# The entries of two graph attentions: a first block of 256 nodes, and Newton's steps of the later blocks on POOL

## The chip, the cores and the metric

The kernel runs on one core of a Trainium2 chip. The metric is the device time of one execution, in microseconds (us); less is better. Five engines work side by side, each through its own list of instructions in order: PE (matmuls), DVE (vector), ACT (activations), POOL (GpSimd) and SP, which here only starts transfers. Between engines there are semaphores. Transfers are started from the queues of SP, ACT and POOL.

## The reference

Four layers, each a graph attention and a feed-forward network, on 2708 nodes of 256 numbers, in float32, with one adjacency matrix for all. The change concerns the graph attentions of layers 2 and 3, which have one head:

```
xn = layernorm(x)                      # per node: mean, variance, 1/sqrt(var + 1e-5)
Wh = xn @ W (+ bias in layer 2)        # 2708 x 256
e  = leaky_relu((Wh @ a1)[:, None] + (Wh @ a2)[None, :], 0.2)
x  = x + softmax(where(adj > 0, e, -9e15)) @ Wh        # elu of it in layer 3
```

The x that enters has just received the results of a mixture of experts: in layer 1 each node is sent to one expert of eight, in layer 2 to two. Their results lie in device memory, and are fetched and added to x, weighted, before the layer norm can start.

## The kernel before

x stays in SBUF as X, 22 tiles of 128 nodes (the last has 20). Both attentions are made by one function, `gat_single` (from L1163). It has an **entry**, which makes everything that the pairs of nodes need, and then the long loop over pairs (`gat_pairs`, L664, and the matmuls of L1311). This loop can start only when the entry has ended, since each of its steps reads `big_p`, a row over all nodes. I call the entry of layer 2 the first entry (tiles `fys`, `g2...`) and that of layer 3 the second (tiles `dys`, `g3...`).

The entry works on six blocks, `chunks(512)`: five of four tiles and one of two (148 nodes). For each block:

- `combine` (L1689) has started the loads of all blocks at the beginning, one transfer `y` for each block and choice (512 KB; whole tiles and the short last tile apart), alternately from SP's and POOL's queue, and for the first block's second choice from ACT's. It then adds the results tile by tile on DVE (L1715): one instruction for each tile in the first entry, two in the second. It is a generator; each `next` adds one block.
- `Stats.sums` (L136): `bn_stats` and `bn_aggr` on DVE for each tile; if asked, ACT's square root of the block's variances (L147). `Stats.roots` (L150) is the reciprocal that follows on DVE.
- `Stats.newton` (L153) makes the inverse root on DVE instead: `inverse_root` (L307) with three instructions for a first guess and three rounds of three (L320 to L322). It is used for blocks 2 and 3 together, and for 4 and 5 together, since ACT has gone from square roots to exponentials by then.
- `norm` (L1191): one DVE instruction for each tile, x minus mean, times rstd, into `f` (L108).
- `project` (L1197): PE transposes the tiles by pairs (L1207), ACT copies them into `ft` and sums them (L1213), PE multiplies by W (L123, `pv`), ACT takes two exponentials of the last column (L1226, L1227), and the 256 columns are scaled into V, by ACT in blocks 0 to 3 (L1229) and by DVE in 4 and 5 (L1232). Then PE makes the row of scores for the block (L1235, `s1p`) and ACT its exponential (L1238, `big_p`).

The order on DVE is written out by hand: `turn` makes each step's instructions follow the last one of the step before (`tc.issue_after`). It is: add 0; sums 0; add 1; roots 0; norm 0; sums 1; add 2; (project 0); roots 1; norm 1; (project 1); sums 2; add 3; sums 3; newton 2+3; norm 2, project 2, norm 3, project 3; add 4; add 5; sums 4+5; newton 4+5; norm 4; norm 5; project 4; project 5. At the end a sum over all nodes (L1283) and a row of V for nodes with no neighbour (L1288, L1289).

POOL has little to do in an entry: it starts its loads, and later it clears a part of the next layer's weights `w` and starts a few loads of weights (L1381, L1766, L93), in the second entry it clears and starts the masks (L2250, L2245) and two loads (L93, L86).

Of the kernel before, what the change touches and what calls it, by code (L numbers as in the profile page):

```python
# [16 lines left out]
P = 128  # L17
N = 2708
# [25 lines left out]
def chunks(width):  # L44

    return [(c, min(width, N - c)) for c in range(0, N, width)]


def tiles_of(start, length):
# [254 lines left out]
        nc.vector.tensor_scalar(net.empty, den, 0.0, None, ALU.is_equal)  # L304


def inverse_root(net, pool, v, scale, eps, name, out=None):  # L307


    nc = net.nc  # L310
    n = v.shape[1]
    x = pool.tile([P, n], F32, name=f"{name}x")
    nc.vector.tensor_scalar(x, v, scale, eps, ALU.mult, ALU.add)
    half = pool.tile([P, n], I32, name=f"{name}h")
    nc.vector.tensor_scalar(half, x.bitcast(I32), 1, None, ALU.logical_shift_right)
    y = pool.tile([P, n], F32, name=f"{name}y") if out is None else out
    nc.vector.tensor_scalar(y.bitcast(I32), half, -1.0, float(0x5F3759DF), ALU.mult, ALU.add)
    t = pool.tile([P, n], F32, name=f"{name}t")
    for _ in range(3):
        nc.vector.scalar_tensor_tensor(t, y, -0.5, y, ALU.mult, ALU.mult)  # L320
        nc.vector.tensor_tensor(t, t, x, ALU.mult)
        last = nc.vector.scalar_tensor_tensor(y, t, 1.5, y, ALU.add, ALU.mult)  # L322
    return y if out is None else last
# [839 lines left out]
def gat_single(net, key, head, feed, elu):  # L1163
# [7 lines left out]
    with ExitStack() as ctx:  # L1171
# [7 lines left out]
        nc.vector.memset(ratio[:, LAST:], 0.0)  # L1179

        nc.scalar.activation(small.tile([P, 1], F32, name="warm", bufs=1), net.ln_eps, AF.Sqrt)
        blocks = chunks(512)
        parts = big.tile([P, NT // 2, 2], F32, name="parts")
        ln = Stats(net)
        with ExitStack() as c1:
# [11 lines left out]
            def project(n):  # L1197
                n0, nw = blocks[n]
                its = tiles_of(n0, nw)
                ft = work.tile([P, 2, 512], F32, name="ft")  # L1200
                for k in range(0, len(its), 2):
                    pair = its[k : k + 2]
                    ps = psum.tile([P, 2, 2 * P], F32, name="tp")
                    for m, t in enumerate(pair):
                        r, f = rows(t), fs.pop(t)
                        for c in range(2):
                            nc.tensor.transpose(  # L1207
                                ps[:, c, m * P : m * P + r], f[:r, c * P : (c + 1) * P], net.ident[:r, :r]
                            )
                    pw = (len(pair) - 1) * P + rows(pair[-1])  # L1210

                    for c in range(2):
                        nc.scalar.activation(  # L1213
                            ft[:, c, k * P : k * P + pw],
                            ps[:, c, :pw],
                            AF.Copy,
                            accum_out=parts[:, 2 * n + k // 2, c : c + 1],
                        )
                    for m, t in enumerate(pair):
                        r = rows(t)  # L1220
                        pv = psum.tile([P, D + 1], F32, name="pv", bufs=3)
                        net.matmul_k(pv[:r], ft[:, :, (k + m) * P : (k + m) * P + r], w)
                        low = V[:r, t, D : D + 1]

                        with tc.issue_after(ln.root.ins) if t == 0 else nullcontext():
                            nc.scalar.activation(low, pv[:r, D:], AF.Exp, scale=SLOPE)  # L1226
                        nc.scalar.activation(ratio[:r, t : t + 1], pv[:r, D:], AF.Exp, scale=1.0 - SLOPE)  # L1227
                        if n < 4:
                            nc.scalar.activation(V[:r, t, :D], pv[:r, :D], AF.Copy, scale=low)  # L1229
                        else:  # L1230
                            with tc.issue_after(last.ins):
                                nc.vector.tensor_scalar(V[:r, t, :D], pv[:r, :D], low, None, ALU.mult)  # L1232
                ps = psum.tile([P, 512], F32, name="s1p")
                for c in range(2):
                    nc.tensor.matmul(  # L1235
                        ps[:, :nw], a1[:, c, :].to_broadcast([P, P]), ft[:, c, :nw], start=c == 0, stop=c == 1
                    )
                nc.scalar.activation(  # L1238
                    big_p[:, n0 : n0 + nw], ps[:, :nw], AF.Exp, scale=1.0 - SLOPE, bias=0.0 if bias is None else head.grow
                )  # L1240

            def tiles(n0, n1):
                return tiles_of(*blocks[n0])[0], tiles_of(*blocks[n1])[-1] + 1
# [10 lines left out]
            def add():  # L1254
                return next(rest, None)

            turn(add)
            turn(ln.sums, *tiles(0, 0))
            turn(add)
            turn(ln.roots, *tiles(0, 0))  # L1260
            turn(norm, 0)
            turn(ln.sums, *tiles(1, 1))
            turn(add)
            project(0)
            turn(ln.roots, *tiles(1, 1))
            turn(norm, 1)
            project(1)
            turn(ln.sums, *tiles(2, 2), root=False)
            turn(add)
            turn(ln.sums, *tiles(3, 3), root=False)  # L1270
            turn(ln.newton, small, *tiles(2, 3))
            for n in (2, 3):
                turn(norm, n)
                project(n)
            turn(add)
            turn(add)
            turn(ln.sums, *tiles(4, 5), root=False)
            turn(ln.newton, small, *tiles(4, 5))
            for n in (4, 5):
                turn(norm, n)  # L1280
            for n in (4, 5):
                project(n)
            nc.vector.tensor_reduce(fsum, parts.rearrange("p n c -> p c n"), AX.X, ALU.add)  # L1283

            one_row = slice(SPARE, SPARE + 1)
# [113 lines left out]
class Routing:  # L1399
# [288 lines left out]

    def combine(self, pool):  # L1689

        net, nc, X = self.net, self.net.nc, self.net.X
        loaded = []
        queues = nc.sync, nc.gpsimd
        for n, (n0, nw) in enumerate(chunks(512)):
            its = tiles_of(n0, nw)
            ys = []
            for c in range(self.choices):
                y = pool.tile([P, 4, D], F32, name=f"y{c}", bufs=len(chunks(512)))
                for k0, k1, r in whole_and_rest(its):
                    r0 = (c * NT + its[k0]) * P  # L1700

                    engine = nc.scalar if n == 0 and c else queues[(n + c) % 2]
                    read = engine.dma_start(
                        y[:r, k0:k1, :],
                        self.ys[r0 : r0 + (k1 - k0 - 1) * P + r, :].rearrange("(t p) d -> p t d", p=r),
                    )
                    if engine is nc.gpsimd:
                        self.read = read
                ys.append(y)
            loaded.append((its, ys))  # L1710
        for its, ys in loaded:
            for k, t in enumerate(its):
                r = rows(t)
                for c, y in enumerate(ys):
                    last = nc.vector.scalar_tensor_tensor(  # L1715
                        X[:r, t, :], y[:r, k, :], self.weight[:r, c, t : t + 1], X[:r, t, :], ALU.mult, ALU.add
                    )
            yield last


def attention(net, route, ln2, router, weights, mixture):
# [629 lines left out]
```

## Time and profile before

| | us |
|---|---|
| runs of the kernel before: median of 3 (lowest, highest) | 2817.94 (2809.52, 2823.55) |
| the profiled execution | 2806.95 |
| its span in the trace | 2805.2 |
| first entry: first add on DVE to first matmul of the pairs | 1350.55 to 1399.70 |
| second entry: the same | 2499.97 to 2551.70 |

| busy over the whole span | PE | DVE | ACT | POOL |
|---|---|---|---|---|
| share | 93% | 52% | 37% | 13% |

PE's share says that the kernel as a whole is bound by PE; the two entries together take about 101 us of the span, and an entry has its own limits: it begins with PE empty, as all of PE's work hangs on additions and layer norms that DVE has to do first. A line of the chain of waits reads: start, duration, what. In a list of instructions the tile that is written stands left of the arrow, those read right of it, then the shape, the count, and in brackets how long the engine was idle before, and whose end it waited for.

### The profile page before, as it was taken

To read this page: it belongs to the slowest core of one execution; us is meant where nothing else is said; L and a number is where in the kernel's file an instruction comes from. 1 tells how busy PE (TensorE), PEld (TensorE's weight loads), DVE (VectorE), ACT (ScalarE), POOL (GpSimd) and SP (SyncE) were. 2 spreads that over 40 slices of the span, in tenths; PEclk is the share of its full clock that TensorE was granted. 3 is DMA by queue.
4 is the path that set the end of the run, shared out by engine and by line. 5 is a ranking of instruction groups with operands and counts; after the bars stand their busy time and mean duration, and the time that the engine had idled before them with its cause. 6 is when DMAs were issued, how large, how long until landed. Compare 5 with 4: busy or idle time off the path is not lost.

```text
span 2805.2 us, 32369 instructions
## 1 busy us (share of the span) xinstructions
PE 2603.2 (93%) x11710; PEld 1611.2 (57%) x11710; DVE 1454.0 (52%) x3102; ACT 1040.9 (37%) x1641; POOL 377.2 (13%) x470
## 2 busy tenths in 40 slices
PE   5999999798999999969799989999989999969998
PEld 4667746574333444558588743333346777757885
DVE  7753348543777776332554456554664222255555
ACT  3444443314565662321444322233332222234453
POOL 1000012100000001134130013323331111110002
PEclk9999999787999999989899999999999999989999
DMA  8899420000000002654310010000121111040001
GB/s 294 287 290 304 149 69 1 3 5 1 1 1 1 1 1 85 173 168 133 108 33 1 1 36 23 18 1 24 77 99 64 35 33 33 25 168 33 1 1 40
DMA packets 106874, 197.70 MB, mean 70 GB/s; under 512 B 8846, under 2 KB 63736, under 8 KB 103876
## 3 DMA queue, kind: packets, MB, share of 16 engines
q1 hardware_dynamic: 88010, 146.82, 16.9%
q0 software_dynamic: 14896, 43.89, 4.8%
q10 hardware_dynamic: 3806, 4.85, 0.6%
q8 instruction: 99, 1.62, 0.2%
q14 instruction: 63, 0.52, 0.1%
HBM read 135.82 MB, written 59.71 MB: 70 GB/s over the span
## 4 chain that ended last, share of the span: by engine, by line
PE 77%; DVE 8%; issue 5%; DMA 4%; ACT 3%; POOL 2%; SPq 0%; ACTq 0%; POOLq 0%; DVEq 0%
PE acc L1311 15%; PE acc L805 8%; PE acc L284 7%; PE h L2031 7%; PE den L816 4%; PE po L2063 4%; PE po L1872 4%; PE score L273 3%; PE sc L1852 3%; PE pv L123 3%; PE h L943 2%; PE sc L1818 2%; PE po L123 2%; DMA dys<-y,to 2%; PE pl L123 1%
## 5 line engine op out<-in xcount | busy, mean ns | idle before, releaser
L675 DVE SCALAR_TENSOR_TENSOR e<-e,mask 128x768 f32<-128x768 f32 (+2 forms) x264 | 412.1, 1576 | 304.4 <-ACT e L674 304.3
L674 ACT ACTIVATE e<-big_p,minus_one,ratio 128x768 f32<-128x768 f32 (+2 forms) x264 | 394.8, 1513 | 367.0 <-PE acc L1311 229.8
L1311 PE MATMUL acc<-V,e 128*128 128x257 f32 (+1 forms) x1936 | 433.5, 383 | 4.5 <-DVE e L675 4.4
L1311 PEld LDWEIGHTS acc<-V,e 128*128 128x128 f32 (+1 forms) x1936 | 352.3, 186 | 85.7 <-issue 32.1
L805 PE MATMUL acc<-e,V 128*64 128x512 f32 (+1 forms) x1056 | 242.7, 548 | 4.4 <-DVE e L675 4.4
L2031 PE MATMUL h<-w,ft 128*128 (+1 forms) x752 | 234.1, 453 | 0.5 <-DVE dso_far L1497 0.5
L284 PE MATMUL acc<-F,e 128*128 128x257 f32 x968 | 226.3, 384 | 3.0 <-DVE e L281 2.6
L284 PEld LDWEIGHTS acc<-F,e 128*128 128x128 f32 x968 | 173.4, 185 | 66.9 <-DVE e L281 28.4
L805 PEld LDWEIGHTS acc<-e,V 128*64 128x64 f32 x1056 | 107.9, 137 | 161.8 <-issue 129.2
L1852 PE MATMUL sc<-qt,kt 64*128 64x512 f32 (+5 forms) x568 | 170.1, 566 | 4.1 <-ACT e L1866 2.4
L2048 DVE TENSOR_TENSOR hh<-hh,h 128x682 f32<-128x682 f32 x47 | 40.7, 865 | 247.5 <-PE h L2031 247.5
L2031 PEld LDWEIGHTS h<-w,ft 128*128 128x128 f32 x752 | 135.9, 191 | 56.5 <-issue 1.8
L1866 ACT ACTIVATE e<-sc 128x1024 f32<-128x1024 f32 (+4 forms) x121 | 100.2, 857 | 183.1 <-PE sc L1852 167.8
L281 DVE TENSOR_TENSOR e<-e,mask 128x512 f32<-128x512 f32 (+2 forms) x132 | 80.4, 625 | 149.0 <-ACT e L275 147.3
L1878 DVE TENSOR_TENSOR sum<-sum,e 128x1024 f32<-128x1024 f32 (+5 forms) x95 | 104.7, 1102 | 74.5 <-ACT e L1866 71.2
L2063 PE MATMUL po<-w,ht 114*128 (+1 forms) x564 | 131.6, 383 | 5.3 <-DVE ht L2056 5.3
L275 ACT ACTIVATE e<-score 128x512 f32<-128x512 f32 (+2 forms) x132 | 69.7, 544 | 179.0 <-PE score L273 152.1
L1872 PE MATMUL po<-e,V 128*64 128x512 f32 (+4 forms) x484 | 112.3, 542 | 17.5 <-DVE e L1870 9.0
L816 PE MATMUL den<-e,low 128*3 128x512 f32 (+1 forms) x1056 | 123.8, 542 | 0.3 <-DVE e L675 0.3
L2063 PEld LDWEIGHTS po<-w,ht 114*128 114x128 f32 x564 | 107.5, 191 | 27.8 <-DVE ht L2056 12.9
L273 PE MATMUL score<-QK 128*128 128x512 f32 (+2 forms) x264 | 112.1, 554 | 1.2 <-ACT e L275 0.7
L1852 PEld LDWEIGHTS sc<-qt,kt 64*128 64x128 f32 (+1 forms) x568 | 58.4, 188 | 89.3 <-issue 74.0
(639 smaller groups left out, 3463.3 us busy)
## 6 DMA issues: line engine op xcount, KB each, us to landing
row<-in_adj SPq DMA_DIRECT2D x21, 1354.0 KB
raw<-in_adjT SPq DMA_DIRECT2D x35, 768.0 KB
hs<-zero SPq DMA_DIRECT2D x8, 2838.0 KB
hidden<-hr SPq DMA_DIRECT2D x32, 256.0 KB
wd<-in_f_wd SPq DMA_DIRECT2D x8, 1024.0 KB
kept<-mask SPq DMA_DIRECT2D x21, 338.5 KB
mask<-kept SPq DMA_DIRECT2D x21, 338.5 KB
w<-in_d_w1T SPq DMA_DIRECT2D x8, 682.0 KB
```

Of the source, the lines that this page charges most:

```text
L123: self.nc.tensor.matmul(out, lhsT[:, c, :], rhs[:, c, :], start=first and c == 0, stop=last and c == n - 1)
L273: nc.tensor.matmul(ps[:r, :iw], QK[:, 0, span(j)], QK[:, 1, i0 : i0 + iw], start=True, stop=True)
L284: nc.tensor.matmul(acc[k][:ri], e[:r, k * P : k * P + ri], F[:r, j, :], start=j == 0, stop=j == NT - 1)
L674: nc.scalar.activation(v, big_p[:, i], AF.Relu, bias=net.minus_one, scale=ratio)
L675: return nc.vector.scalar_tensor_tensor(v, v, 1.0, net.mask[:, j, i], ALU.add, ALU.mult)
L805: made = nc.tensor.matmul(acc[n][half, :iw], V[:, j, h, :], e[:, k, i0 : i0 + iw], start=j == 0, stop=j == NT - 1)
L816: made = nc.tensor.matmul(den[g : g + Q, :iw], low[:, j, h, Q - 1 - q : 2 * Q - 1 - q], e[:, k, i0 : i0 + iw], start=False, stop=j == NT - ...
L1311: nc.tensor.matmul(acc[k][:ri], e[:, k * P : k * P + ri], V[:, j, :], start=j == 0, stop=j == NT - 1)
L1852: nc.tensor.matmul(by_pairs(ps[:r, g])[:, :, o:], kt[b, span(j)], qt[b, :, o:iw], start=True, stop=True)
L1872: nc.tensor.matmul(by_pairs(po[b])[:, :, o:], V[:r, j, g, :], by_pairs(e[:r, g])[:, :, o:], start=j == 0, stop=j == last,)
L2031: last = nc.tensor.matmul(halves[s, n][:, q, :HALF], fts[s][:, c, :], weights.w13[n][:, es[s], c, q * HALF : (q + 1) * HALF], start=c == 0 ...
L2063: last = nc.tensor.matmul(po, ht[:KP, k, :], w2[:KP, es[s], k, :], start=k == 0, stop=k == KC - 1)
```

## The change

A list of blocks `ENTRY` replaces `chunks(512)` in the entry and in `combine`: 256 nodes, four blocks of 512, and the last 404. So there are again six blocks: tiles 0-1, 2-5, 6-9, 10-13, 14-17, 18-21. The generator of additions now stops after each pair of tiles, so a block of four takes two steps. Blocks 0 and 1 keep ACT's square root. From block 2 on each block has its own inverse root, whose guess (three instructions) is on DVE and whose three rounds, now of four instructions each, are on POOL, since `inverse_root` gets `steps=nc.gpsimd`. It returns the guess, so that the next step on DVE is ordered behind the guess and not behind the rounds; `norm` waits for the rounds by its data. V is scaled by ACT in all blocks but the last.

The new order on DVE is: add tiles 0-1; sums 0; add 2-3; roots 0; norm 0; add 4-5; sums 1; add 6-7; (project 0); roots 1; norm 1; add 8-9; (project 1); then for block 2 and for block 3: sums, guess, add, add, norm, project; for block 4: sums, guess, add, add, then sums and guess of block 5, norm 4, project 4; norm 5, project 5.

```diff
+ENTRY = [(0, 256)] + [(c, min(512, N - c)) for c in range(256, N, 512)]
...
-def inverse_root(net, pool, v, scale, eps, name, out=None):
+def inverse_root(net, pool, v, scale, eps, name, out=None, steps=None):
...
-    nc.vector.tensor_scalar(y.bitcast(I32), half, -1.0, float(0x5F3759DF), ALU.mult, ALU.add)
+    guess = nc.vector.tensor_scalar(y.bitcast(I32), half, -1.0, float(0x5F3759DF), ALU.mult, ALU.add)
     t = pool.tile([P, n], F32, name=f"{name}t")
+    if steps:
+
+        for _ in range(3):
+            steps.tensor_tensor(t, y, y, ALU.mult)
+            steps.tensor_tensor(t, t, x, ALU.mult)
+            steps.tensor_scalar(t, t, -0.5, 1.5, ALU.mult, ALU.add)
+            steps.tensor_tensor(y, y, t, ALU.mult)
+        return guess
     for _ in range(3):
...
-        blocks = chunks(512)
+        blocks = ENTRY
...
-                            accum_out=parts[:, 2 * n + k // 2, c : c + 1],
+                            accum_out=parts[:, pair[0] // 2, c : c + 1],
...
-                        if n < 4:
+                        if n + 1 < len(blocks):
                             nc.scalar.activation(V[:r, t, :D], pv[:r, :D], AF.Copy, scale=low)
...
+            def roots(n):
+
+                t = slice(*tiles(n, n))
+                return inverse_root(net, small, ln.mv[:, t, 1], 1.0, LN_EPS, "nr", ln.rstd[:, t], nc.gpsimd)
+
             turn(add)
             turn(ln.sums, *tiles(0, 0))
             turn(add)
             turn(ln.roots, *tiles(0, 0))
             turn(norm, 0)
+            turn(add)
             turn(ln.sums, *tiles(1, 1))
             turn(add)
             project(0)
             turn(ln.roots, *tiles(1, 1))
             turn(norm, 1)
+            turn(add)
             project(1)
-            turn(ln.sums, *tiles(2, 2), root=False)
-            turn(add)
-            turn(ln.sums, *tiles(3, 3), root=False)
-            turn(ln.newton, small, *tiles(2, 3))
-            for n in (2, 3):
+            for n in range(2, len(blocks) - 1):
+                turn(ln.sums, *tiles(n, n), root=False)
+                turn(roots, n)
+                turn(add)
+                turn(add)
+                if n + 2 == len(blocks):
+                    turn(ln.sums, *tiles(n + 1, n + 1), root=False)
+                    turn(roots, n + 1)
                 turn(norm, n)
                 project(n)
-            turn(add)
-            turn(add)
-            turn(ln.sums, *tiles(4, 5), root=False)
-            turn(ln.newton, small, *tiles(4, 5))
-            for n in (4, 5):
-                turn(norm, n)
-            for n in (4, 5):
-                project(n)
+            turn(norm, len(blocks) - 1)
+            project(len(blocks) - 1)
...
-        for n, (n0, nw) in enumerate(chunks(512)):
+        for n, (n0, nw) in enumerate(ENTRY):
...
-                y = pool.tile([P, 4, D], F32, name=f"y{c}", bufs=len(chunks(512)))
+                y = pool.tile([P, 4, D], F32, name=f"y{c}", bufs=len(ENTRY))
...
-            yield last
+                if k % 2:
+                    yield last
```

As built, the other stages keep their instructions and order. In the two entries the order on the queues changes as follows. On POOL each of the twelve instructions of an inverse root waits for the one before it by POOL's own semaphore. In the first entry, block 5's rounds stand on POOL behind the clearing of `w` and the load `ln`, and the loads `wv`, `wk` and `wq` stand between their first four instructions. In the second entry two loads (`w`, `b`) stand ahead of block 5's rounds. On SP, in the second entry, the order of the loads becomes block 0, block 2, block 1, block 3 and so on (before: 0, 1, 2, 3); on POOL block 1, block 3, block 2, and so on (before: 1, 2, 3).

## The prediction

> **What bounds the kernel now.** By the page PE is busy 93% of the span, so time can be had where PE waits. I read stretches of time first, then the chain of waits, then the lists of the engines. Stretches of the second entry (columns: stretch, length, PE, PEld, DVE, ACT and POOL busy, granted PE clock, DMA share, GB/s):
>
> ```profile
> 2494.60:2508.50 13.90, 0.00 (x0) 0.00 (x0) 8.49 (x27) 0.30 (x1) 7.55 (x9) 0.52 0.91 329
> 2508.50:2549.20 40.70, 37.44 (x157) 26.22 (x158) 33.30 (x119) 24.70 (x112) 1.32 (x2) 0.95 0.58 215
> ```
>
> For 13.9 us PE has nothing, then it is nearly full until the entry ends. The chain of waits shows the same in its kinds of steps:
>
> ```profile
> 2499.97 3.25 DVE X L1715 x8
> ...
> 2504.89 3.22 DVE X L1715 x8
> 2508.12 0.10 DVE rstd L151
> ...
> 2511.28 3.22 DVE X L1715 x8
> ...
> 2515.19 0.41 PE tp L1207 x2
> ...
> 2526.99 3.66 PE pv L123 x16
> 2530.65 1.73 PE s1p L1235 x4
> ```
>
> First DVE decides, up to 2515; then PE, whose blocks of four tiles end every 6.5 to 6.8 us (s1p at 2530.65, 2537.16, 2543.66). The first entry is alike: s1p ends every 6.6 us. So there are two clocks to keep: PE's (6.6 us a block) and DVE's. DVE's prices for four tiles, from starts in its list: additions 1.58 (first entry; 3.16 in the second, which has two choices), sums 1.75, norm 1.30, reciprocal 0.20; two tiles half of it. An inverse root on DVE is twelve instructions:
>
> ```profile
> 1366.96 0.17 DVE L313 TENSOR_SCALAR nrx<-mv 128x8 f32<-128x8 f32 x1
> ...
> 1367.58 0.17 DVE L320 SCALAR_TENSOR_TENSOR nrt<-rstd 128x8 f32<-128x8 f32 x1
> ...
> 1369.39 2.67 DVE L108 TENSOR_SCALAR f<-X,mv,rstd 128x256 f32<-128x256 f32 x8
> ```
>
> 2.43 us from L313 to L108, 0.62 of it the guess. Two such sets make 4.9 us an entry; after the change DVE keeps four guesses, 2.4 us. From a norm's start to PE's first transpose I take 0.5 (one norm of 0.42 and a signal).
>
> **The change, part by part. 1: the smaller first block.** Additions, sums, additions, reciprocal, norm stand before PE's start; with two tiles each this is 2.5 us shorter in the first entry, 4.1 in the second. But the second additions need block 1's transfer, and that isn't made smaller. What the queues had moved by 1352.9 (first entry) and by 2502.6 (second; q1 is SP, q0 POOL, q10 ACT; packets, MB, share):
>
> ```profile
> q1 hardware_dynamic: 1153, 1.15, 52.6%
> q0 software_dynamic: 141, 0.54, 22.8%
> ```
>
> ```profile
> q1 hardware_dynamic: 1044, 1.05, 38.0%
> q0 software_dynamic: 183, 0.69, 20.1%
> q10 hardware_dynamic: 528, 0.52, 17.3%
> ```
>
> POOL's queue starts at 1351.0 and has block 1's 0.52 MB through at 1352.9; block 0's data were through 0.7 us before DVE took them, so block 1 is there at 1353.6. DVE, ready at about 1351.4, waits. Then: additions to 1354.4, reciprocal 1354.6, PE starts at 1355.1 (before: 1356.17), 1.1 us won, not 2.5. In the second entry SP now loads block 2 ahead of block 1's second half: 1.31 MB instead of 1.05, less 0.26 that block 0 saves on ACT's queue; by those rates I put it at 2503.3, additions end at 2504.45, PE starts at 2505.15 (before 2508.55): 3.4 us won.
>
> **2: PE's blocks.** Block 0 took 10.7 and 10.4 us before, four tiles at half clock; two tiles I take at 7.0. Then 6.6 a block, and 6.4 for the last (1.04 + 0.27 + 3.74 + s1p 1.72 x 404/512). Unhindered that is 1355.1 + 7.0 + 4 x 6.6 + 6.4 = 1394.9 against 1397.15 before.
>
> **3: the rounds on POOL.** No row shows a small arithmetic instruction on POOL. Rows of larger ones (mean ns):
>
> ```profile
> L1824 POOL TENSOR_TENSOR qt<-qt,tmp 128x512 f32<-128x512 f32 x10 | 13.0, 1300 | 38.3 <-DVE tmp L1823 38.3
> L1824 POOL TENSOR_TENSOR qt<-qt,tmp 128x148 f32<-128x148 f32 x2 | 1.0, 496 | 6.9 <-DVE tmp L1823 6.9
> L2198 POOL TENSOR_TENSOR X<-X,b 128x256 f32<-128x256 f32 x21 | 15.8, 773 | 247.6 <-DVE f L108 247.6
> L1308 POOL TENSOR_TENSOR X<-X,late 128x256 f32<-128x256 f32 x21 | 19.9, 985 | 25.9 <-issue 25.9
> ```
>
> With 1265 for the undisturbed 512 wide (kt) and 497 for 148, an element costs 2.1 ns and 4 elements 0.19 us. Each step waits for the one before: POOL's memset L725, which waits for L728, starts 0.06 after its end; the load L2245 starts 0.29 after L2250. So a step costs 0.19 to 0.48; I take 0.27, since arithmetic is nearer to the memset than to a load. Beside DVE both suffer: L1308, beside L675, takes 0.21 more than L2198, and L675's 128x768 rows take 1305 ns there against 956 later. I add 0.21 to steps beside the additions: 4 of 12 in the first entry, 8 of 12 in the second. A set of rounds costs 4 x 0.48 + 8 x 0.27 = 4.1 us in the first, 8 x 0.48 + 4 x 0.27 = 4.9 in the second. It was 1.8 on DVE.
>
> The Trainium skill ("SBUF — State Buffer", "Who interferes with whom") says that the port pair that DVE and GpSimd share is locked for whole instructions. By it a step beside additions would wait out one of 0.395, sets cost 4.8 and 6.4, and the sum below were about +12 instead of +5.5. The rows agree in kind; no row here shows the full lock.
>
> **4: the sum.** Norm of a block waits for its rounds; sums of the next block stand behind this norm on DVE. So from block 2 DVE's period is norm 1.3 + sums 1.75 + guess 0.6 + rounds + 0.2 for two signals: 7.95 in the first entry, 8.75 in the second, both over PE's 6.6. What the additions cost beside the rounds (1.6, 3.2) is covered by them; the rounds themselves have no cover.
>
> First entry: guess of block 2 ends at 1363.25; PE could begin block 2 at 1368.05 (it is free at 1368.7), block 3 at 1376.0, block 4 at 1383.95. Block 5's rounds stand behind the memset L1381 (1.8) and one load (0.75) and have three loads of 0.73 among them: 1383.35 + 2.55 + 3.24 + 2.2 + 0.6 = 1391.9. It ends at 1398.3: +1.15. Second entry: guess of block 2 at 2515.65, PE at 2521.25, 2530.0, and 2540.15 for block 4, where DVE is late itself (additions, sums and guess of block 5 stand before norm 4). Block 4 ends at 2546.75, block 5 at 2553.15, against 2549.17: +4.0. `big_p` of 404 instead of 148 adds 0.2 each. V on ACT in block 4 costs nothing (0.81 us a tile under PE's 0.87). Sum: +5.5 us; the profiled execution's 2806.95 becomes 2812.5. That execution lies 11.0 under the median of 2817.94, so I put the difference on the median: **2823.4**.
>
> **Rivals. The rounds are hidden:** a step costs 0.19 and DVE doesn't hinder it (2.3 a set). Then PE decides in the first entry, -2.25 + 0.2, and DVE's additions in the second (PE at 2519.3, 2526.1, 2535.35; end 2548.35), -0.8 + 0.2: -2.6 in all, 2815.3. For it: such steps touch only 4 columns. Against it: L1308 and L675.
>
> **The steps are dear**, the other side: 0.48 a step, 0.69 beside additions. Sets of 6.6 and 7.4; the same chain gives +11.4 and +10.8, 22 in all, 2840. It decides, that is it passes 0.5% (14.1 us), from 0.38 a step undisturbed. For it: twelve waits in a row on an engine whose smallest rows with a wait differ by 0.06 to 0.29.
>
> **The clock falls:** PE waits 2.5, 2.1 and 3.5 us in the second entry. Before, the granted clock fell 2.1 us after the last matmul at 1342.9, and 5.0 after that at 2490.3, and came back 5.9 and 3.7 us after the start. A fall costs about 3 (block 0's 10.5 against 6.6); three make +14.5, 2832.
>
> The skill ("TensorE: Matmul & The Clock Gate", "HAM oscillation") puts the limit at idle gaps of about 3.4 us; by it one of the three waits would count, +8.5. The 2.1 us seen here says that less can be enough.
>
> **How the numbers follow.** Forecast 0.45, hidden 0.25, dear 0.20, clock 0.07, something else that wins 0.03. 0.5% is about what a measurement of this kernel can tell from no change. Forecast and hidden lie within it, dear beyond, clock on the edge: faster 0.03, same 0.74, slower 0.23. The runs of before scatter by 6 to 8 about their median; from 2815.3 less some of this, to the dear case: 2811 to 2840.
>
> **What would show it.** PE's first transposes near 1355.1 and 2505.2 on the time axis of before; DVE waiting for `y` of block 1; spacing of POOL's steps 0.27 alone and 0.48 beside additions; norms of blocks 2 and 3 released by POOL; block periods of 8 and 8.8 us. Wrong if the steps are spaced by over 0.38, if norms find rstd ready, or if the clock falls between blocks.

## The result, and the profile after

| | before | after |
|---|---|---|
| median of 20 runs each, side by side, us | 2818.02 (2806.98 to 2825.46) | 2825.57 (2811.45 to 2831.09) |
| ratio to before, 95% interval | | 1.0023 (1.0012 to 1.0034) |
| profiled execution: time / span, us | 2806.95 / 2805.2 | 2819.24 / 2817.5 |
| first entry, from POOL's first load of `y` to the first `acc`, us | 53.03 | 53.44 |
| second entry, the same, us | 56.15 | 61.50 |

The changed kernel is slower by 0.23%, some 6.5 us; the forecast was 5.5 us and a median of 2823.4. The two profiles differ by 12.3 us, and that is not the size of the change: 4.7 us of it lie ahead of the first entry, where both programs are the same, and 1.7 between the last scatter of `dys` (POOL's last write of the experts' results to device memory) and POOL's loads behind it (6.29 us against 4.58; 4.48 to 6.29 over the profiles in which POOL loads `y`). So every entry below is measured within itself, from POOL's first load of `y` to the first `acc`, PE's first matmul of the pairs: together +5.8 us. The rows at both ends, first of before, then of after (start, us, engine, line, operation):

```profile
1346.67 2.69 POOL L1703 DMA_DIRECT2D y<-fys  x4 [2.06 <-DMA fys<-ys,to]
1399.70 8.48 PE L1311 MATMUL acc<-V,e 128*128 128x257 f32 x38 [1.59 <-DVE e L675]
2495.55 4.17 POOL L1703 DMA_DIRECT2D y<-dys  x6 [3.62 <-DMA dys<-y,to]
2551.70 14.54 PE L1311 MATMUL acc<-V,e 128*128 128x257 f32 x66 [1.59 <-DVE e L675]
```

```profile
1351.39 2.90 POOL L1720 DMA_DIRECT2D y<-fys  x4 [2.05 <-DMA fys<-ys,to]
1404.83 3.49 PE L1327 MATMUL acc<-V,e 128*128 128x257 f32 x15 [1.73 <-DVE e L687]
2502.48 4.40 POOL L1720 DMA_DIRECT2D y<-dys  x6 [5.32 <-DMA dys<-y,to]
2563.98 2.19 PE L1327 MATMUL acc<-V,e 128*128 128x257 f32 x9 [1.64 <-DVE e L687]
```

The expectations of e1 to e4 count from the last scatter instead; take 3.0 off for a first entry, 6.3 off for a second one that is derived from after, and 4.6 for one that is derived from before. One run of e2 (5251 us) and one of e4 (3061 us) lie far above the others of their kernel and are left out of the ratios.

The same two stretches of the second entry as shown for before (columns: stretch, length, PE, PEld, DVE, ACT and POOL busy, granted PE clock, DMA share, GB/s):

```profile
2501.60:2513.60 12.00, 0.00 (x0) 0.01 (x1) 4.92 (x16) 0.30 (x1) 7.80 (x9) 0.50 0.90 330
2513.60:2561.40 47.80, 41.40 (x157) 28.31 (x158) 34.36 (x116) 25.74 (x113) 14.13 (x50) 0.89 0.53 196
```

The stretch without PE is 1.9 us shorter, the one with PE is 7.1 longer, at a clock of 0.89 instead of 0.95, and PE stands still in 6.4 of its 47.8 us. Before, it stood still in 3.3 of 40.7. The chain of waits of the changed kernel (start, us, what) says who decides:

```profile
2512.07 0.88 DVE X L1732 x2
...
2523.97 0.18 DVE rstd L321
2524.23 0.37 POOL nrt L326
...
2528.28 0.21 POOL rstd L329
2528.52 1.38 DVE f L112 x4
...
2545.78 0.64 DVE f L112
2546.47 1.40 PE tp L1219 x8
2547.87 5.34 PE pv L127 x16
2553.21 1.73 PE s1p L1247 x4
```

Before, PE took the chain over at block 1. Now it goes through DVE, POOL's twelve steps and back to DVE twice, and PE comes in with block 4 only. PE's own list shows the same from its side (start, us, line, operation, tiles; in brackets how long PE was idle before, and for what):

```profile
2528.98 1.41 PE L1219 MATMUL tp<-ident,f 128*128 128x128 f32 x8 [1.55 <-DVE f L112]
...
2537.10 1.41 PE L1219 MATMUL tp<-ident,f 128*128 128x128 f32 x8 [1.34 <-DVE f L112]
2538.43 3.74 PE L127 MATMUL pv<-g3w,ft 128*128 128x257 f32 x16
...
2546.47 1.40 PE L1219 MATMUL tp<-ident,f 128*128 128x128 f32 x8 [2.58 <-DVE f L112]
2547.79 5.42 PE L127 MATMUL pv<-g3w,ft 128*128 128x257 f32 x16
```

PE waits before blocks 2, 3 and 4, and after the longest of these waits the same 16 products take 5.42 us instead of 3.74: the granted clock was down, which I call a fall, as two windows of that time show (clock: third number from the end):

```profile
2540.20:2546.40 6.20, 3.69 (x14) 2.13 (x12) 6.09 (x23) 2.72 (x11) 4.51 (x14) 1.00 0.00 0
2546.40:2552.40 6.00, 5.93 (x22) 4.53 (x23) 2.34 (x8) 2.95 (x15) 2.92 (x13) 0.72 0.29 67
```

What a step costs on POOL is read from the starts in its list. Two beside DVE's additions, two after them:

```profile
2525.85 0.32 POOL L326 TENSOR_TENSOR nrt<-rstd 128x4 f32<-128x4 f32 x1
2526.25 0.32 POOL L327 TENSOR_TENSOR nrt<-nrt,nrx 128x4 f32<-128x4 f32 x1
...
2527.44 0.20 POOL L326 TENSOR_TENSOR nrt<-rstd 128x4 f32<-128x4 f32 x1
2527.72 0.20 POOL L327 TENSOR_TENSOR nrt<-nrt,nrx 128x4 f32<-128x4 f32 x1
```

0.40 apart beside additions, 0.28 alone. (One addition on DVE takes 0.40 too; whether the steps keep its pace or have this price by themselves, these rows don't tell.) A set takes 3.8 us in the first entry and 4.3 in the second. DVE's list of the first entry shows the wait for a set, and something that no step of the prediction had:

```profile
1379.06 1.38 DVE L112 TENSOR_SCALAR f<-X,mv,rstd 128x256 f32<-128x256 f32 x4 [2.35 <-POOL rstd L329]
...
1386.72 3.06 DVE L112 TENSOR_SCALAR f<-X,mv,rstd 128x256 f32<-128x256 f32 x4
1394.64 1.37 DVE L112 TENSOR_SCALAR f<-X,mv,rstd 128x256 f32<-128x256 f32 x4 [4.86 <-POOL rstd L329]
```

Norm 4 did not wait (the sums and the guess of block 5 stand before it), but its four instructions took 3.06 us instead of 1.38. POOL's list of that moment:

```profile
1386.48 0.20 POOL L329 TENSOR_TENSOR rstd<-rstd,nrt 128x4 f32<-128x4 f32 x1
1386.81 1.80 POOL L1397 MEMSET w<- 32x2048 f32 x1
1388.56 0.81 POOL L1784 DMA_DIRECT2D ln<-in_d_ln  x1
1389.43 0.19 POOL L326 TENSOR_TENSOR nrt<-rstd 128x4 f32<-128x4 f32 x1
1389.57 0.72 POOL L97 DMA_DIRECT2D wv<-in_d_wvT  x1
```

The memset of the next layer's weights lies on top of norm 4, and loads lie between the first steps of block 5's set. The first of the four norms took 2.04 and ended 0.15 after the memset; the other three, beside the load `ln`, took some 0.4 each as always.

### The profile page after: what moved, and what is told of

It is laid out like the page before. It is cut to its first block, busy times and chain, and to the rows that moved or that the text cites. A ratio compares the mean times of both kernels' runs of the same rounds, so it can differ in the third digit from the quotient of the medians.

```text
span 2817.5 us, 32437 instructions
## 1 busy us (share of the span) xinstructions
PE 2613.4 (93%) x11710; PEld 1613.9 (57%) x11710; DVE 1451.9 (52%) x3074; ACT 1044.3 (37%) x1645; POOL 402.2 (14%) x566
## 4 chain that ended last, share of the span: by engine, by line
PE 76%; DVE 8%; issue 5%; DMA 4%; ACT 3%; POOL 3%; SPq 0%; ACTq 0%; POOLq 0%; DVEq 0%
PE acc L1327 15%; PE acc L817 8%; PE acc L288 7%; PE h L2049 7%; PE den L828 4%; PE po L2081 4%; PE po L1890 4%; PE score L277 3%; PE sc L1870 3%; PE h L955 2%; PE pv L127 2%; PE sc L1836 2%; PE po L127 2%; DMA dys<-y,to 2%; PE pl L127 1%
## 5 line engine op out<-in xcount | busy, mean ns | idle before, releaser
L288 PEld LDWEIGHTS acc<-F,e 128*128 128x128 f32 x968 | 173.4, 185 | 67.0 <-DVE e L285 28.5
L2066 DVE TENSOR_TENSOR hh<-hh,h 128x682 f32<-128x682 f32 x47 | 40.7, 866 | 247.5 <-PE h L2049 247.5
```

The lines of the kernel that those rows point to most:

```text
L288: nc.tensor.matmul(acc[k][:ri], e[:r, k * P : k * P + ri], F[:r, j, :], start=j == 0, stop=j == NT - 1)
```

## The experiments

All edits are on the changed kernel, unless said otherwise. The table has every run; the entries are those of the one profile of each, the ratio is over its runs.

| | first entry | second entry | ratio to before, 95% |
|---|---|---|---|
| before | 53.03 | 56.15 | |
| after | 53.44 | 61.50 | 1.0023 (1.0012 to 1.0034) |
| e1 rounds on DVE | 55.54 | 65.86 | 1.0045 (1.0029 to 1.0062) |
| e2 POOL alone | 56.34 | 58.58 | 1.0027 (1.0017 to 1.0037) |
| e3 norm 0 first | 53.95 | 60.40 | 1.0012 (0.9997 to 1.0026) |
| e4 one round | 49.46 | 57.12 | 1.0017 (1.0004 to 1.0029) |
| e5 sums ahead | 49.95 | 59.49 | 0.9998 (0.9985 to 1.0011) |
| e6 POOL's other work late | 51.72 | 61.09 | 1.0022 (1.0008 to 1.0036) |
| e7 e3, e5 and e6 together | 48.45 | 57.96 | 0.9992 (0.9975 to 1.0009) |
| e8 paired on DVE, norm 0 first | 51.97 | 61.14 | 1.0003 (0.9988 to 1.0018) |
| e9 blocks alone | 51.15 | 60.78 | 1.0013 (0.9998 to 1.0028) |
| e10 `y` in order | 47.90 | 61.63 | 1.0011 (0.9995 to 1.0027) |
| e11 first entry only | 48.93 | 56.11 | 0.9989 (0.9972 to 1.0006) |
| e12 PE kept busy | 55.35 | 59.98 | 1.0025 (1.0010 to 1.0039) |

(In e10 POOL loads no `y`; its entries count from 3.02 and 4.60 us after the last scatter.)

**e1: the rounds back on DVE, block by block.**

```
-                return inverse_root(net, small, ln.mv[:, t, 1], 1.0, LN_EPS, "nr", ln.rstd[:, t], nc.gpsimd)
+                return inverse_root(net, small, ln.mv[:, t, 1], 1.0, LN_EPS, "nr", ln.rstd[:, t])
```

> The changed kernel with the twelve steps of each later block back on DVE as nine (the new blocks and the new order kept). Each entry is measured from the start of the last scatter of fys or dys to the first acc of the pairs: 56.05 and 60.73 us before, 56.45 and 67.79 after. Theory A (each block's rounds cost by themselves: one set per block instead of one per two blocks, and no cover for them on either engine): a set on DVE is 1.8 us where the norm now waits 2.35 (first entry) or 1.22 (second) for POOL, so norms 2 and 3 come 0.55 earlier each in the first and 0.6 later each in the second; norm 4 stands behind two sets, 3.6 us later than now less what the memset cost it. About 57.4 and 72.6, that is 5 to 6 us slower than after. Theory B (it is POOL that is slow, the blocks are harmless): both entries at or below those of before, 7 or more us faster than after.

Theory A. The new blocks with a set each on DVE are slower than with POOL. DVE works without a pause, and PE waits 2.70 us before block 2 and 5.93 before block 4, with two falls of the clock:

```profile
2527.80 1.82 PE L1219 MATMUL tp<-ident,f 128*128 128x128 f32 x8 [2.70 <-DVE f L112]
2529.41 4.78 PE L127 MATMUL pv<-g3w,ft 128*128 128x257 f32 x16
...
2549.11 1.75 PE L1219 MATMUL tp<-ident,f 128*128 128x128 f32 x7 [5.93 <-DVE f L112]
```

So POOL does relieve DVE. What costs is that there are four sets an entry instead of two: e9, the same blocks with two paired sets on DVE, is 4.4 and 5.1 shorter.

**e2: POOL alone, on the kernel before.**

```
-            turn(ln.newton, small, *tiles(2, 3))
+            turn(roots, 2, 3)
...
-            turn(ln.newton, small, *tiles(4, 5))
+            turn(roots, 4, 5)
```

> The kernel before with its two sets of rounds of each entry (eight and six tiles wide) on POOL and nothing else changed: blocks of 512, its order, one set per two blocks. Theory A: a set on POOL alone takes 12 x 0.28 + 0.2 = 3.6 against 1.8 on DVE. In the first entry norm 2 has 3.1 us to spare before PE wants it and norm 4 5.8, so nothing: 56.05. In the second norm 2 has none (PE waited 0.84 for it) and norm 4 0.2: 1.8 + 1.6 = 3.4 later, 64.1. In all +3.4 on before. Theory B (moving the rounds to POOL carries the whole loss): +7 on before.

(One thing more differs from before: ACT scales V of block 4 too, as in the changed kernel. PE waits for ACT in blocks 4 and 5 no longer than before.)

5.7 us in all, between the theories. A set of eight tiles alone took 3.4 us (12 steps of 0.28) as A had it, and the second entry lost 2.4, near A's 3.4. The first lost 3.3 where A had nothing, and not by DVE: norm 2 came 1.5 us later than before, well ahead of the end of block 1. But in this program PE's list has the first transpose of block 2 ahead of the last products and the `s1p` of block 1, and PE does its list in order:

```profile
1370.28 0.33 PE L1219 MATMUL tp<-ident,f 128*128 128x128 f32 x1 [2.45 <-DVE f L112]
1370.44 2.48 PE L127 MATMUL pv<-g2w,ft 128*128 128x257 f32 x8
1372.71 3.04 PE L1247 MATMUL s1p<-ft,g2a 128*128 128x512 f32 x4
```

Before, the products came first and `s1p` took 1.88; here the clock fell in a wait that the block did not need. The slack that A counted was there, the order of the list gave it away.

**e3: norm 0 ahead of block 1's additions.**

```
             turn(ln.sums, *tiles(0, 0))
-            turn(add)
             turn(ln.roots, *tiles(0, 0))
             turn(norm, 0)
             turn(add)
+            turn(add)
```

> The changed kernel with the two additions of block 1 (first half) moved behind norm 0, so that PE's start no longer waits for block 1's transfer (the two exponentials of block 0 are kept behind both square roots on ACT, as now). PE starts about 2.6 us earlier in the first entry and 4.5 in the second. Theory A (from block 2 on DVE and its waits for POOL set the end): only the 0.9 us of reciprocal and norm 0 that no longer stand behind the wait for y reach the end: 55.5 and 66.9, 1.8 faster than after. Theory B (the start that was not won is what costs): 53.9 and 63.3, 7 faster than after.

PE's first transpose came 2.7 and 4.1 us earlier, and the entries changed by +0.5 and -1.1. Theory A: PE's start does not set the end. What was won there is spent before block 1 and block 2, and it costs clock (the second entry):

```profile
2518.22 1.66 PE L1219 MATMUL tp<-ident,f 128*128 128x128 f32 x8 [1.97 <-DVE f L112]
2519.67 5.08 PE L127 MATMUL pv<-g3w,ft 128*128 128x257 f32 x16
```

**e4: one round instead of three on POOL.**

```
-        for _ in range(3):
+        for _ in range(1):
             steps.tensor_tensor(t, y, y, ALU.mult)
```

> The changed kernel with one of Newton's three rounds (four of twelve steps) on POOL, two rounds left out, so that a set takes 1.3 us and its wait goes. Theory A (the wait for the rounds is on the path): first entry 3.0 less (PE's waits of 0.88 and 2.50 go, less what the memset may still hold up), second 2.4 less (two waits of norm of 1.22; PE's wait before block 4 stays, since the sums and the guess of block 5 stand before norm 4): 53.4 and 65.4, 5.5 faster than after. Theory B (the steps are hidden, and the time goes to the transfers and the order): no change on after.

In the entries theory A, and more: 4.0 and 4.4 less. In the whole run little of it is seen: the ratio is 0.06% under that of after, 1.7 us, with intervals of 0.12% on both. The profile of e4 has 7.4 us more between its first `acc` and the last scatter of `dys` (1098.7 against 1091.4), in instructions that the edit does not touch: PE stayed at half clock where after has full speed from 1825 on (columns as above).

```profile
1816.00:1821.00 5.00, 5.00 (x15) 1.69 (x14) 0.00 (x0) 0.00 (x0) 3.78 (x5) 0.50 0.31 109
1821.00:1836.00 15.00, 14.09 (x25) 3.60 (x26) 5.81 (x5) 2.60 (x3) 1.65 (x2) 0.50 0.05 18
```

Of the fourteen profiles, before, after, e1 and e12 have 1091 to 1094 us between the entries, the other ten 1098 to 1101. In all ten the clock is 0.50 from 424 to 434 us after the first `acc`, in the four it is 1.00. Whether a shorter entry makes this longer fall likelier is not settled: there is one profile of each kernel. It is one reason why small gains in an entry are hard to find in the ratio (see the end).

**e5: sums and guess one block ahead.**

```
-                turn(ln.sums, *tiles(n, n), root=False)
-                turn(roots, n)
+                if n == 2:
+                    turn(ln.sums, *tiles(n, n), root=False)
+                    turn(roots, n)
                 turn(add)
                 turn(add)
-                if n + 2 == len(blocks):
-                    turn(ln.sums, *tiles(n + 1, n + 1), root=False)
-                    turn(roots, n + 1)
+                turn(ln.sums, *tiles(n + 1, n + 1), root=False)
+                turn(roots, n + 1)
```

> The changed kernel with one thing moved: for every block from 2 on the sums and the guess of the next block stand ahead of the norm (as the changed kernel does for the last pair only), so that POOL has additions, sums and guess of the next block (3.9 us in the first entry, 5.5 in the second) in which to do a set of rounds. Theory A (the norm's wait for the rounds is the loss): the waits of 2.35 and 1.22 go, periods fall to DVE's own work of 5.4 (first, so PE's 6.6 decides) and 6.9 (second); norm 2 of the second entry comes 1.1 later, norm 4 2.4 earlier. First entry 3.4 less, second 2.4 to 4 less than after, 6 to 7 faster in all, back at the time of before. Theory B (it is contention on POOL and DVE, so that more work beside the rounds stretches both): the waits shrink by less than half, within 2 of after.

Theory A: 3.5 and 2.0 less, 5.5 together; the ratio fell by 0.25%, 7 us. Norms 2 to 4 no longer wait for POOL, and follow each other by 5.3 to 6.4 us in the first entry and 6.8 to 6.9 in the second (starts 2530.63, 2537.44, 2544.33), although POOL's steps run beside more work of DVE. What is left in the second entry is the wait before block 2, made longer as expected:

```profile
2531.09 1.75 PE L1219 MATMUL tp<-ident,f 128*128 128x128 f32 x7 [3.45 <-DVE f L112]
```

**e6: POOL's other work out of the way** (first entry).

```
-        nc.gpsimd.memset(self.w2[96:, :, KC - 1, :], 0.0)
+        with net.tc.issue_after(net.biased.ins):
+            nc.gpsimd.memset(self.w2[96:, :, KC - 1, :], 0.0)
...
-        wv, wk, wq = (net.load_weight(wp, a[f"d_w{n}T"], f"w{n}") for n in "vkq")
+        with net.tc.issue_after(net.rooted.ins):
+            wv, wk, wq = (net.load_weight(wp, a[f"d_w{n}T"], f"w{n}") for n in "vkq")
```

(`net.biased` is POOL's last addition of the bias, `net.rooted` the last step of the last set; `ln` moves with the weights.)

> The changed kernel with POOL's other work of the first entry moved: the memset of w (1.80 us) behind POOL's additions of the bias in the pairs, the loads ln, wv, wk, wq behind the last set of rounds. Theory A (in the first entry the memset holds up norm 4, 3.06 us for four instead of 1.38, and with it PE, which waits 2.50 for block 4; block 5's rounds behind memset and loads end late, but PE comes to block 5 later still): norm 4 takes 1.4, PE's wait falls from 2.50 to 0.8, the first entry is 1.7 shorter, the second unchanged. Theory B (norm 4 is long because of the rounds that run beside it): no change.

Theory A to the tenth: norm 4 takes 1.41, PE's wait for block 4 is 0.87, the first entry 1.7 shorter.

```profile
1380.21 1.41 DVE L112 TENSOR_SCALAR f<-X,mv,rstd 128x256 f32<-128x256 f32 x4
```

```profile
1380.71 1.41 PE L1219 MATMUL tp<-ident,f 128*128 128x128 f32 x8 [0.87 <-DVE f L112]
```

So it was the memset, not the rounds, that held norm 4 (e6 moves the loads too, but the norms beside `ln` in after had their usual time). The ratio can't resolve 1.7 us (0.06%), and doesn't show it.

**e7: e3, e5 and e6 together** (the three edits above, nothing else).

> Three edits together on the changed kernel: sums and guess one block ahead (e5), norm 0 ahead of block 1's additions (e3), POOL's other work of the first entry late (e6). Theory A: in the first entry no norm is late any more, PE decides from its start, 2.7 us earlier than in after: about 48 to 49 from POOL's first load of y to the first acc, against 53.4 in after and 53.0 before. In the second DVE decides with 6.9 a block: 56.5 to 58 against 61.5 and 56.2. In all 7 to 9 faster than after, 1 to 4 faster than before. Theory B (PE's start cannot be used, since block 1 then waits for its transfer and the clock falls in that wait): first entry no better than before.

Theory A: 48.45 and 57.96. The first entry is 4.6 under before, the second 1.8 over it, since PE still waits 2.13 and 2.52 us before blocks 1 and 2, at half clock afterwards. The ratio of 0.9992 is 0.31% under that of after; against before it is no difference that can be measured.

**e8: the new blocks, norm 0 first, paired rounds on DVE.**

```
-            for n in range(2, len(blocks) - 1):
...
+            for n in (2, 4):
+                if n == 4:
+                    turn(add)
+                    turn(add)
+                turn(ln.sums, *tiles(n, n), root=False)
+                turn(add)
+                turn(add)
+                turn(ln.sums, *tiles(n + 1, n + 1), root=False)
+                turn(ln.newton, small, *tiles(n, n + 1))
+                for m in (n, n + 1):
+                    turn(norm, m)
+                    project(m)
```

> The new blocks without POOL: norm 0 ahead of block 1's additions, and Newton's rounds on DVE, one set of eight tiles for two blocks as before the change (so two sets of 2.4 us an entry). Theory A (the sets, not the blocks, are what cost): first entry 50 to 51, PE waits about 1 for block 2; second 57, PE waits about 3 for block 2 and 1.4 for block 4; 5 to 6 faster than after, about 1 faster than before. Theory B (the smaller first block moves the wait from the start to later blocks and wins nothing): both entries at those of before, 53 and 56.

In the ratio as A said, 0.20% faster than after. In the entries much less: the first is 52.0, 1.5 under after (PE waits 2.08 for block 2, and the clock falls), but the second is 61.1, no better than after: waits of 2.81 and 3.97 before blocks 1 and 2, both at half clock. The expectation had left the clock out. That its ratio is so good with this second entry is not explained by its profile.

**e9: the blocks alone** (the loop of e8 without the edit of e3).

> The smaller first block alone: the new blocks and the changed kernel's start (additions of block 1 ahead of norm 0), Newton's rounds on DVE with one set for two blocks, as before the change. Times from POOL's first load of y to the first acc (before 53.0 and 56.2, after 53.4 and 61.5). Theory A (PE starts a little earlier, but has two tiles less to do before it wants block 2, whose norm stands behind a paired set on DVE): in the first entry PE waits about 1.5 for block 2, 51.5 in all; in the second about 5, and the clock falls in it, 61 to 62. Theory B (the loss of the second entry belongs to POOL's rounds, not to the blocks): second entry at 54 to 56.

Theory A in both: 51.2 and 60.8, though the wait of 1.5 in the first entry did not appear. Without a single step on POOL the second entry loses 4.6 of the 5.35 us, in one wait:

```profile
2536.34 1.75 PE L1219 MATMUL tp<-ident,f 128*128 128x128 f32 x7 [4.83 <-DVE f L112]
```

PE starts earlier and has two tiles instead of four in block 0, so it is ready for block 2 at 24.1 us after POOL's first load (30.0 before). DVE still has the additions and a paired set to do before norm 2, which comes at 28.5 (29.6 before).

**e10: the loads of `y` in the order of need**, on e7.

```
-        queues = nc.sync, nc.gpsimd
+        queues = nc.sync, nc.scalar
...
-                    engine = nc.scalar if n == 0 and c else queues[(n + c) % 2]
+                    engine = queues[c if self.choices == 2 else n % 2]
```

> The kernel of e7 with the loads of y issued so that no later block's load runs beside an earlier one's on another queue: all first choices on SP and all second choices on ACT (second entry), blocks in turn on SP and ACT (first entry), none on POOL. Theory A (block 1 lands late because loads of blocks 2 to 5 on POOL's queue share the same engines, which are full, 1.05 in the windows): DVE's wait for y of block 1, 1.53 in the second entry, goes, norm 1 comes 2 earlier, PE's waits of 2.13 and 2.52 fall to under 1 and 2, the second entry ends 2 to 4 earlier, 54 to 56; the first hardly changes, 48. Theory B (all loads together are limited by the engines, and two queues in order end no sooner than three): both entries as in e7, 48.5 and 58.

The first entry has no wait for `y` after the first addition, and ends 0.5 earlier than in e7. The second can't be read: another wait took the place. ACT's queue had seven loads to issue, that took 12.63 us, and block 0's square root stood behind them in ACT's list (start, us, engine, line):

```profile
2497.54 12.63 ACTq L1721 DMA_DIRECT2D y<-dys  x7
2510.22 0.30 ACT L151 ACTIVATE sd<-mv,ln_eps 128x2 f32<-128x2 f32 x1 [13.81 <-DMA y<-dys]
```

PE started 5.8 us later than in e7. Which of the theories holds for the transfers of the second entry stays open.

**e11: the first entry of e7, the second of before.**

```
-        blocks = ENTRY
+        blocks = chunks(512) if bias is None else ENTRY
```

(with the order of before and its additions of four tiles in the second entry)

> The first entry as in e7 (small first block, rounds on POOL a block ahead, norm 0 first, POOL's other work late), the second entry as before the change (blocks of 512, paired rounds on DVE). Theory A (the change pays where an addition is 0.4 us a tile and DVE has time to spare, and costs where it has two choices to add): 48.5 and 56.2, 4.6 faster than before, ratio 0.998. Theory B (what is won in the entry is given back later, since the clock falls elsewhere): no faster than before, although the first entry is.

The entries as A said, 48.93 and 56.11, 4.1 under before. The ratio of 0.9989 fits 4.1 us and fits nothing as well: its interval holds 1. It is the fastest version in the entries, and no version here beats the kernel before by more than can be measured.

**e12: PE kept busy in its waits** (second entry).

```
+                with tc.issue_after(end.ins):
+                    for _ in range(0 if bias is not None else (0, 1, 1, 2, 0, 0)[n]):
+                        warm = psum.tile([P, 2, 2 * P], F32, name="tp")
+                        for k in range(8):
+                            nc.tensor.transpose(warm[:, k % 2, :P], net.ident, net.ident)
```

(`end` is the last matmul of `s1p`.)

> The changed kernel with work for PE in the three waits of the second entry: 8 transposes of the identity (1.04 us, nobody reads them) after blocks 1 and 2, 16 after block 3, where PE waits 1.55, 1.34 and 2.58 in after. Nothing else changes, and DVE's chain does not see it. Theory A (a wait of about 2 us or more lets the granted clock fall to 0.5, and the fall costs 1.7 us: block 4's 16 pv took 5.42 in place of 3.74): no wait is longer than 0.6, the clock stays at 1.00, every set of pv takes 3.74; second entry 61.5 less 1.7 = 59.8. Theory B (the fall after the wait of 2.58 has another cause, since the wait of 2.50 in the first entry of after had none): falls appear as before, 61.5.

Theory A: block 4's products take 3.74 after a wait of 0.92, and the second entry is 1.5 shorter. (The wait before block 2 was 1.71, not under 0.6 as expected; no fall followed it.)

```profile
2540.82 1.91 PE L1254 MATMUL tp<-ident 128*128 128x128 f32 x16
2543.66 1.31 PE L1219 MATMUL tp<-ident,f 128*128 128x128 f32 x8 [0.92 <-DVE f L112]
2544.89 3.74 PE L127 MATMUL pv<-g3w,ft 128*128 128x257 f32 x16
```

In the same profile the first entry, whose code is that of after, fell into the clock after the very wait of 2.50 that had no fall in after, and was 1.9 us longer (0.5 of it at its start):

```profile
1385.55 1.80 PE L1219 MATMUL tp<-ident,f 128*128 128x128 f32 x8 [2.50 <-DVE f L112]
1387.15 4.86 PE L127 MATMUL pv<-g2w,ft 128*128 128x257 f32 x16
```

So whether a wait of this length costs 1.4 us more differs between executions of the same code; what decides it is not shown. In the ratio e12 is no better than after.

## Why the prediction was right, point by point

The sum was right (+5.5 forecast, +5.8 in the entries of the two profiles, +6.5 by the ratio), and so was the mechanism: rounds without cover, norms released by POOL, DVE's period over PE's. The terms were less good, and errors cancelled: 1.7 of the 5.8 us are a fall of the clock that the sum did not have, and without it the entries would have been 4.1 longer. That the size was met so closely is partly luck.

- **1, the smaller first block.** The first entry's PE started 1.6 us earlier (1.1 predicted), the second's 2.1 (3.4 predicted; its 2508.55 for PE's start before is 2508.80 in the trace). The step that failed is "by those rates I put it at 2503.3", the landing of block 1's second half in the second entry, 7.75 after POOL's first load. It took the bytes of a queue for the landing of a transfer. In after SP had moved 1.33 MB, more than the 1.31 that were counted, 7.05 us after POOL's first load, but DVE's wait for this half ended at 9.59. It mattered little: e3 starts PE 2.7 and 4.1 us earlier still, and the end hardly moves.
- **2, PE's blocks.** 6.6 to 6.7 a block, as predicted. Block 0 took 7.0 in the second entry, 5.7 in the first (7.0 predicted).
- **3, the rounds.** 0.28 a step alone (0.27 predicted). Beside additions it was 0.40, not 0.48: this term was mis-sized. A set is 3.8 and 4.3 instead of 4.1 and 4.9. The rival by which steps are dear, and the sum of +12 for a full lock, fall with the same rows.
- **4, DVE's period.** 7.7 and 8.1 us from norm 2 to norm 3 (7.95 and 8.75 predicted, the difference is the set's). That the waits of norms 2 and 3 are on the path is shown by e5, which only covers them and takes 5.5 us off the entries, and by e4. "Norms of blocks 2 and 3 released by POOL" was seen in both entries.
- **4, block 5 of the first entry.** The predicted extra wait of 1.35 did not reach PE: norm 5 waited 4.86 for POOL, but PE came to block 5 without a wait, because block 4 had been made late by what the prediction had not seen, the memset on top of norm 4 (1.68 us; e6 takes 1.7 off). +1.35 predicted with `big_p`, +0.4 found.
- **4, block 4 of the second entry.** PE began it 44.0 us after POOL's first load, 44.6 predicted. Then came the fall of the clock, 1.68, that the sum had not. +4.2 predicted, +5.35 found.
- **The rival of the falling clock** came true beside the forecast, not in its place: one fall in the profile of after, at 1.7 us and not 3. The price had been taken from block 0, where all of PE's work and ACT's start lie in the slow time. A fall between blocks was also one of the prediction's signs of being wrong; here the errors the other way made up for it.
- **The rival of hidden rounds** did not occur; e4 shows what it would have given in the entries, 8.4 less than after. The prediction's 2815.3 for it is 8.1 less than its forecast.
- What the prediction did not say is which part costs what. By e9 the blocks alone are worth -1.9 and +4.6, by e2 POOL alone, with paired sets, +3.3 and +2.4 (the first of these by PE's list). They don't add up: together they cost +0.4 and +5.35. The second entry loses by the smaller first block already.

## What to carry to other kernels

A shorter first block pays only if the engine behind it can keep the following blocks coming: compare the periods first (here DVE's 6.9 us of own work in the second entry against PE's 6.6), and not only the start. Moving a chain of small steps to an idle engine needs cover for its whole length on the engine that waits; putting the next block's sums ahead of the waiting norm gave the 5.5 us back without making a step faster. Before work goes to an idle engine, look at what else it has queued there, and on which instructions of the others that work will fall.

## What the runs showed of the hardware

- **POOL's memset stops DVE's norm.** A memset of 32x2048 (1.80 us) on POOL, 0.09 after norm 4's start, lengthened DVE's norms from 1.38 to 3.06 for four; without it 1.41 (e6). In e3 and e12 it lies there again, and the norms take 3.06 again. In e5 it falls on the first instruction of a guess, a `tensor_scalar` as the norms are, which takes 1.38 instead of 0.17. Before, and in e1, e2, e8 and e9, it falls on DVE's sums, and they take no longer. The Trainium skill ("SBUF — State Buffer", "Who interferes with whom") says that `tensor_scalar`, which a norm is, can run in a two-port mode, and that DVE in this mode and GpSimd then shut each other out for a whole instruction; the 3.06 agrees. The prediction had weighed this page against the additions only: there the steps were drawn out by 0.12 each, and none waited out a whole addition.
- **The clock falls after waits of 2 us.** In the entries of after and e1 to e12 PE waited 13 times between 1.97 and 2.58 us before a block; in 11 of these the products that followed were slow (16 `pv` up to 5.42 instead of 3.74), in two not (2.50 in after, 2.36 in e4). All eight longer waits (2.70 to 5.93) had it, of the shorter ones just one (1.46 in e3, soon after another fall). In 16 of these 20 falls the granted clock was 0.50 for 3.41 us, and PE's instructions took 1.0 to 1.7 us longer; in four it was down for 6.83 us, and they took 1.3 to 2.6 longer. (After the 2.36 of e4 it stayed at 1.00.) In after the clock changes at 2500.53, 2521.01, 2548.32 and 2551.73, all multiples of 3.41 us apart; where a wait lies between such points differs from one execution to the next, and this may be why the same wait has a fall or none, which no run here tests.
  The Trainium skill ("TensorE: Matmul & The Clock Gate", "HAM oscillation") puts the limit at gaps of some 3.4 us; here shorter gaps were enough.
- **The time of a run follows its mean clock.** The 20 runs of after go from 2811.45 us at 0.964 to 2831.09 at 0.956. This scatter, and the 7 to 10 us of the slow stretch near 1820, are larger than the effect of this change. A line through time and mean clock, fitted to the runs of e1 to e12 and of before beside them, gives 2.3 us for 0.001 of clock. At the same clock after is 4.4 over before (± 1.2), and e4 is 0.6 under it, e7 3.0 and e11 4.8 (each ± 1.5). In the entries these were 5.8 over, of which 1.7 are the fall, and 2.6, 2.8 and 4.1 under. So most of what the entries win or lose is in the runs, and the clock hides it. This comparison leaves out what a kernel loses by its own clock, so it does not make e7 or e11 faster in time.
- **Issuing loads can hold an engine for long.** Seven loads of `y` held ACT's list for 12.6 us in e10, while one load had taken it 0.46.
